# Layer 0's product of batches 1 to 3 on four column groups, with the row sums taken from added-up weights and the maximum in a PSUM bank of its own

## The chip, the core and the metric

The kernel runs on one core of a Trainium2 chip. A core has five engines that run side by side, each through its own list of instructions in order: PE (TensorE, matrix products into PSUM), DVE (VectorE), ACT (ScalarE), POOL (GpSimd) and SP (SyncE, here only for issuing DMAs). They wait for each other through semaphores. PSUM, the memory that PE writes, has 8 banks of 2 KB in each of 128 partitions. The metric is the device time of one execution in microseconds, the median of a few runs; a profiled execution also gives a trace of every instruction.

## What is computed

All data is fp32. `x` has 4 batches of 256 tokens with 512 features, and each batch has a context of 1601 rows of 512. Two layers follow each other, each a cross attention and a feed-forward step, all added onto `x`:

```python
x = x + _L0_xattn_ref(_layernorm(x), ctx_4096, ...)   # latent attention, 16 heads of 32
x = x + _L0_ffn_ref(_layernorm(x), ...)               # int4 weights, dequantized
x = x + _L1_xattn_ref(_layernorm(x), ctx_4096, ...)   # 16 heads of 96, 4 key/value heads
x = x + _L1_ffn_ref(_layernorm(x), ...)               # low-rank experts, gated
```

The change lies in layer 0's attention:

```python
C_kv = K @ Wkv_d                                      # context rows -> 32 latents
scores = einsum('bnhl,bkl->bhnk', CqWqk, C_kv) / sqrt(32)
attn = softmax(scores)
out = einsum('bhnk,bkhd->bnhd', attn, (C_kv @ Wv_u) per head)
```

The kernel uses that the keys' latents are shared by all heads: per head it forms `latents^T @ weights` (32 by 256) and only then multiplies by `Wv_u`. The softmax's sums come from the same product, with columns of ones beside the latents.

## The kernel before, in words

**Heads.** There are 4 batches times 16 heads in each of two layers, 128 heads in all, and each runs the same steps in `Head.schedule`. The 1601 context rows of layer 0 are 13 tiles of 128 (the last one overlaps, and its repeated rows are masked to zero); layer 1 has 15, with the 256 tokens themselves. The tiles of a head lie in four groups (4, 4, 3, 2 for layer 0, order `ORDER0`; 4, 4, 4, 3 for layer 1), each a tile `S` of up to 128 by 4 by 256 of which 8 exist, enough for two heads.

**Steps of a head.** PE writes scores to PSUM (layer 0: `Head0.score_units`, L1406; layer 1: L1483), four matmuls of 32 rows at a time on four row groups of the array. ACT copies each group to `S` (L1272). DVE takes running maxima over the tiles (L1290, L1293, L1298) into `mx`. PE transposes `mx` (L1321, the "turn") into a PSUM tile `om`, DVE reduces it to one maximum per query (L1325), PE transposes that back, broadcast over all partitions (L1334, the "spread"), into the other half of the same tile, and DVE copies it to SBUF as `mB` (L1342). DVE subtracts `mB` from each of the four groups (L1351), ACT exponentiates them (L1360), and PE multiplies them with the values (layer 0: L1433, layer 1: L1508), accumulating in the first half of `om`. ACT copies the result out (layer 0: `oT`, L1450; layer 1: L1547 to L1553).

**Layer 0's product.** The stationary operand of a tile is 64 wide: 32 latents and 32 ones (`ckv`). Even tiles go to columns 0 to 63 of the array, odd tiles to 64 to 127, so two matmuls stand side by side: 13 matmuls in 7 steps. `l0_output` (L778) adds the two halves up by multiplying `oT` with `wv_h`, which holds `Wv_u` at rows 0 and 64 and a one at rows 32 and 96 to pick the sums; DVE divides (L789, L790) and POOL adds to `x` (L808).

**PSUM.** Scores have two tiles of two banks (`s_psum`), `om` has two tiles of one bank (`o_psum`, tag "o"), and all other products two of one bank (`aux_psum`).

**Order of the work.** Nothing runs in the order in which the program names it. Every step is a `task` with an engine, an assumed duration, dependences, a priority and the buffers that it takes; `Plan.forward` places tasks one at a time where they can start earliest, the priority deciding between equals, and `Plan.order` repeats that with priorities computed backwards and keeps the best of nine rounds. The `AT_` constants shift the first round's priorities of each kind of step; `HOLD` is added to a PE task whose tiling of the array ("form": full, 32 rows, 64 columns, ...) is not the one in use. The result is a fixed list for each engine. `LINE` sets the order of heads: 16 of layer 0 of batch 0; then three stages that mix the 16 layer-1 heads of a batch with the 16 layer-0 heads of the next; then the 16 layer-1 heads of batch 3. Beside the heads PE makes keys (L895), values (L837), queries (L986), output products (L1096) and the feed-forward products (L610).

**Start.** ACT's queue issues loads of `x`, small weights and `wv_h` (L262 to L308) ahead of its first computation (L513); POOL sets constants (L255 to L345) ahead of its first power (L486), which the first layer norm waits for.

## Time and profile before

| what | us |
|---|---|
| median of 3 runs | 1981.87 (1981.84 to 1982.26) |
| the profiled execution | 1979.79 |
| its span, first to last instruction | 1978.0 |
| PE busy in it | 1905.7 (96%), 14745 matmul records |
| DVE busy | 1379.7 (70%), 2086 instructions |
| ACT busy | 1158.3 (59%) |
| POOL busy | 119.4 (6%) |
| mean granted TensorE clock | 0.982 |

One fp32 matmul of the program leaves two records in the trace, so 26 records of a layer-0 product are its 13 matmuls. A group row gives line, engine, operation, output and inputs, shapes and count, then busy time and mean duration in ns, then the idle time of the engine just before such instructions and what ended it. A timeline row gives start and length in us and merges neighbours of one line. A window row gives the length of a stretch, and for each engine its busy time and number of instructions in it.

### The profile page before, as it was taken

To read this page: it belongs to the slowest core of one execution; us is meant where nothing else is said; L and a number is where in the kernel's file an instruction comes from. 1 tells how busy PE (TensorE), PEld (TensorE's weight loads), DVE (VectorE), ACT (ScalarE), POOL (GpSimd) and SP (SyncE) were. 2 spreads that over 40 slices of the span, in tenths; PEclk is the share of its full clock that TensorE was granted. 3 is DMA by queue.
4 is the path that set the end of the run, shared out by engine and by line. 5 is a ranking of instruction groups with operands and counts; after the bars stand their busy time and mean duration, and the time that the engine had idled before them with its cause. 6 is when DMAs were issued, how large, how long until landed. Compare 5 with 4: busy or idle time off the path is not lost. (4 is left out here: it accounts for less than half of the span.)

```text
span 1978.0 us, 35851 instructions
## 1 busy us (share of the span) xinstructions
PE 1905.7 (96%) x14745; PEld 1336.7 (68%) x14745; DVE 1379.7 (70%) x2086; ACT 1158.3 (59%) x1752; POOL 119.4 (6%) x171
## 2 busy tenths in 40 slices
PE   6999899999999998999999999999999999999976
PEld 4566677666767776666666786666676678777743
DVE  3987458888887355888887636588879655577743
ACT  3887356776776434667776533567677654455530
POOL 1001200000001000000000100000000010000000
PEclk9999999999999999999999999999999999999986
DMA  7000432211000315220101024212100012221121
GB/s 196 16 12 28 149 86 57 62 38 36 23 9 23 86 54 151 54 62 28 38 15 30 22 65 142 79 50 57 41 25 17 23 46 57 68 70 45 45 60 42
DMA packets 132871, 109.11 MB, mean 55 GB/s; under 512 B 69059, under 2 KB 110179, under 8 KB 132324
## 3 DMA queue, kind: packets, MB, share of 16 engines
q1 hardware_dynamic: 125332, 96.01, 17.6%
q10 hardware_dynamic: 7376, 10.82, 1.7%
q8 instruction: 116, 1.90, 0.4%
q14 instruction: 47, 0.39, 0.1%
HBM read 93.50 MB, written 13.27 MB: 54 GB/s over the span
## 5 line engine op out<-in xcount | busy, mean ns | idle before, releaser
L1272 ACT COPY S<-s 128x1024 f32<-128x1024 f32 (+2 forms) x512 | 447.5, 905 | 300.4 <-PE s L1483 150.0
L1360 ACT ACTIVATE S<-S 128x1024 f32<-128x1024 f32 (+2 forms) x512 | 472.7, 950 | 156.2 <-DVE S L1351 128.8
L1351 DVE TENSOR_TENSOR S<-S,mB 128x1024 f32<-128x1024 f32 (+2 forms) x512 | 544.9, 1109 | 4.4
L1293 DVE TENSOR_TENSOR mx<-mx,S 128x512 f32<-128x512 f32 (+1 forms) x704 | 464.2, 659 | 113.4 <-ACT S L1272 87.2
L1508 PE MATMUL o<-S,v 128*97 128x256 f32 x1920 | 458.6, 382 | 0.6 <-ACT S L1360 0.6
L1508 PEld LDWEIGHTS o<-S,v 128*97 128x97 f32 x1920 | 302.2, 164 | 107.4 <-issue 22.9
L1483 PE MATMUL s<-q,kT_k_ps_c 32*128 32x256 f32 x4320 | 276.3, 383 | 0.0
L1483 PEld LDWEIGHTS s<-q,kT_k_ps_c 32*128 32x128 f32 x4320 | 224.6, 185 | 44.8 <-issue 19.5
L1433 PE MATMUL o<-S,ckv 128*64 128x256 f32 x1664 | 225.2, 389 | 1.5 <-ACT S L1360 1.3
L1433 PEld LDWEIGHTS o<-S,ckv 128*64 128x64 f32 x1664 | 117.0, 137 | 92.5 <-issue 31.2
L1290 DVE TENSOR_TENSOR mx<-S 128x512 f32<-128x512 f32 x128 | 88.7, 693 | 123.7 <-ACT S L1272 123.4
L837 PE MATMUL v_ps<-wvT_sb,ctxT 128*128 128x192 f32 x832 | 160.4, 336 | 0.0
L895 PE MATMUL k_ps_c<-ctxT,wk_sb 128*128 128x384 f32 (+1 forms) x480 | 159.2, 453 | 0.3 <-ACT kTlast_k_ps_c L905 0.3
L837 PEld LDWEIGHTS v_ps<-wvT_sb,ctxT 128*128 128x128 f32 x832 | 136.8, 192 | 22.5 <-issue 15.5
L1406 PE MATMUL s<-q,ckvT 32*128 32x256 f32 x1664 | 148.6, 409 | 0.0
L1406 PEld LDWEIGHTS s<-q,ckvT 32*128 32x128 f32 x1664 | 90.6, 185 | 54.7 <-issue 34.7
L1325 DVE TENSOR_REDUCE m<-o 128x2 f32<-128x256 f32 x128 | 53.5, 418 | 85.5 <-PE o L1321 84.8
L895 PEld LDWEIGHTS k_ps_c<-ctxT,wk_sb 128*128 128x128 f32 x480 | 79.1, 190 | 40.8 <-issue 13.7
L1096 PE MATMUL wo_ps<-wo,oT 128*128 128x512 f32 x192 | 93.6, 609 | 13.1 <-POOL oT L1083 13.1
L905 ACT COPY kT_k_ps_c<-k_ps_c 32x384 f32<-32x384 f32 (+1 forms) x180 | 76.7, 426 | 47.3 <-PE k_ps_c L895 44.8
L986 PE MATMUL q_ps<-xnT_xn_tp_a,wq 128*128 128x256 f32 x384 | 97.6, 386 | 1.9 <-ACT p_q_ps L995 1.9
L1483 PE MATMUL s<-q,kTlast_k_ps_c 32*128 32x256 f32 x1440 | 96.3, 391 | 0.0
(139 smaller groups left out, 1339.1 us busy)
## 6 DMA issues: line engine op xcount, KB each, us to landing
q<-q_rows SPq DMA_DIRECT2D x192, 96.0 KB
wq<-in_wqT SPq DMA_DIRECT2D x48, 192.0 KB
wo<-in_woT SPq DMA_DIRECT2D x16, 576.0 KB
q<-q_rows SPq DMA_DIRECT2D x128, 64.0 KB
ctxT<-in_ctxT ACTq DMA_DIRECT2D x6, 1024.0 KB
q_rows<-p_q_ps SPq DMA_DIRECT2D x48, 128.0 KB
q<-q_rows SPq DMA_DIRECT2D x192, 32.0 KB
rb<-rsums SPq DMA_DIRECT2D x16, 288.0 KB
```

The costliest lines, as they stand in the source:

```text
L837: nc.tensor.matmul(ps[:, : 2 * HD], lhsT=src.tile[:, c, a : a + P], rhs=wvT_sb[:, c, half * 2 * HD : (half + 1) * 2 * HD], start=(c == 0), ...
L895: nc.tensor.matmul(out, lhsT=wk_sb[:, c, i, :], rhs=rhs, start=(c == 0), stop=(c == NC - 1),)
L986: nc.tensor.matmul(ps[:, :T], lhsT=wq.tile[:, c, :], rhs=xnT.tile[:, c, :], start=(c == 0), stop=(c == NC - 1),)
L1096: nc.tensor.matmul(ps, lhsT=oT.tile[:, i, q * P : (q + 1) * P], rhs=wo.tile[:, i, :], start=(i == 0), stop=(i == G - 2),)
L1272: nc.scalar.copy(S4[g].tile[:, :n, :], self.scored(ps[g].tile, g))
L1293: nc.vector.tensor_tensor(mx.tile[:, :w, :], mx.tile[:, :w, :], t[:, a : a + w, :], ALU.max)
L1351: nc.vector.tensor_tensor(s[:, :n, :], s[:, :n, :], mb.tile[:, None, :].to_broadcast([P, n, T]), ALU.subtract,)
L1360: nc.scalar.activation(s[:, :n, :], s[:, :n, :], AF.Exp, scale=self.scale)
L1406: nc.tensor.matmul(pss[2 * step + r // 2][:, 2 * (r % 2) + s % 2, :], lhsT=st8[self.b]["ckvT"].tile[part, s, :], rhs=qr[part, self.h % 2, ...
L1433: nc.tensor.matmul(po[64 * par : 64 * par + 64, :], lhsT=s["ckv"].tile[:, t, :, :].rearrange("p o l -> p (o l)"), rhs=self.S[g].tile[:, i, :],
L1483: nc.tensor.matmul(pss[2 * step + r // 2][:, 2 * (r % 2) + slot % 2, :], lhsT=s["kT", self.kv].tile[part, c, slot, :], rhs=s["q1", self.kv ...
L1508: nc.tensor.matmul(po[:VW, :], lhsT=s["v", j // 2].tile[:, t, j % 2, :], rhs=self.S[g].tile[:, i, :], start=(k == 0), stop=(k == NK1 - 1),)
```

## The change

For batches 1 to 3 (`Head0.packed`) layer 0's product uses four column groups of 32. Three of them take the latents of three tiles at a time; 13 tiles make five steps (`units_of_three`). The fourth takes ones as the stationary operand, and as the moving operand a tile of weights in which several tiles have been added up: `add_up` puts the sum of groups 0 and 1 into the two free slots of group 3 (`S[3]`, slots 2 and 3), and tiles 8, 9 and 10 into the free slot of group 2; `TERMS` names the five operands (tiles 11 and 12 go in as they are) and which addition each must wait for. That makes 18 matmuls in 5 steps for 13 in 7, and five new DVE additions for each head. `l0_output` then needs a second set of `Wv_u`, `wv_3`, with rows 0, 32 and 64, beside `wv_2`. Batch 0 keeps the old product.

For all 128 heads the turn and the spread go to a PSUM tile of their own (tag "m", one), the product to another (tag "o", now one), and the four subtractions read the spread maximum from PSUM; the copy to `mB` is gone. Priorities are rounded, `HOLD` is 2.0, all `AT_` constants are new, and there is one more, `AT_SUM`, for the additions. Two blocks of definitions only move to another place; they are left out here.

```diff
@@ -66,7 +66,7 @@
     SWITCH = 0.2
-    HOLD = 1.0
+    HOLD = 2.0
     def __init__(self):
         self.tasks = []
...
@@ -74,7 +74,7 @@
     def task(self, eng, us, what, deps=(), prio=0.0, new=(), uses=(), lag=0.0, form="full"):
-        t = Task(eng, us, what, [d for d in deps if d is not None], prio, new, len(self.tasks))
+        t = Task(eng, us, what, [d for d in deps if d is not None], round(prio, 4), new, len(self.tasks))
         t.lag, t.form = lag, form
         for b in (*new, *uses):
             b.users.append(t)
...
@@ -243,11 +243,19 @@
     def s_psum(name):
         return psum.tile([P, 4, T], F32, tag="s", bufs=2, name=name)
+    def m_psum(name):
+        return psum.tile([P, 2, T], F32, tag="m", bufs=1, name=name)
     def o_psum(name):
-        return psum.tile([P, 2, T], F32, tag="o", bufs=2, name=name)
+        return psum.tile([P, 2, T], F32, tag="o", bufs=1, name=name)
     def aux_psum(name):
         return psum.tile([P, 512], F32, tag="aux", bufs=2, name=name)
+    FULL = S // P
+    DUP = (FULL + 1) * P - S
...
@@ -302,13 +310,18 @@
     first_ctx = load_ctx(0, nc.sync, load_wv)
-    wv_h = const.tile([P, H0, 33], F32, name="wv_h")
-    nc.gpsimd.memset(wv_h, 0.0)
-    for r in (0, 64):
-        nc.scalar.dma_start(
-            out=wv_h[r : r + L0, :, 0:32], in_=wv_u.rearrange("l (h d) -> l h d", d=32)
-        )
-        nc.gpsimd.memset(wv_h[r + 32 : r + 33, :, 32:33], 1.0)
+    wv_h = []
+    for name, rows, picks in (("wv_2", (0, 64), (32, 96)), ("wv_3", (0, 32, 64), (96,))):
+        w = const.tile([P, H0, 33], F32, name=name)
+        nc.gpsimd.memset(w, 0.0)
+        for r in rows:
+            nc.scalar.dma_start(
+                out=w[r : r + L0, :, 0:32], in_=wv_u.rearrange("l (h d) -> l h d", d=32)
+            )
+        for r in picks:
+            nc.gpsimd.memset(w[r : r + 1, :, 32:33], 1.0)
+        wv_h.append(w)
...
@@ -778,7 +787,7 @@
                 nc.tensor.matmul(
                     ps[:, (2 * q + j) * 33 : (2 * q + j + 1) * 33],
                     lhsT=oTs[j].tile[:, q * P : (q + 1) * P],
-                    rhs=wv_h[:, 2 * pair + j, :],
+                    rhs=wv_h[Head0.packed(b)][:, 2 * pair + j, :],
                     start=True,
                     stop=True,
                 )
...
@@ -1208,26 +1217,27 @@
-    AT_KEYS = -4.0
-    AT_VALUES = -3.0
-    AT_HALF = 1.5
-    AT_QUERY = -3.2
-    AT_LATENT = -2.8
-    AT_START0 = -5.4
-    AT_W0 = 0.6
-    AT_OUT = -2.0
-    AT_EVICT = -0.2
-    AT_SCORES = -3.0
-    AT_COPY = -0.9
-    AT_MAX = -1.8
-    AT_TURN = -0.9
-    AT_SPREAD = -0.5
-    AT_SUB0 = -0.8
-    AT_SUB1 = -1.0
-    AT_EXP0 = -0.2
-    AT_EXP1 = -0.4
-    AT_PROD = 0.2
-    AT_FIN = -2.8
+    AT_KEYS = -2.9
+    AT_VALUES = -0.2
+    AT_HALF = 1.7
+    AT_QUERY = -7.6
+    AT_LATENT = -9.3
+    AT_START0 = -16.1
+    AT_W0 = -4.1
+    AT_OUT = 0.9
+    AT_EVICT = 1.6
+    AT_SCORES = -2.5
+    AT_COPY = 4.3
+    AT_MAX = -4.3
+    AT_TURN = -2.8
+    AT_SPREAD = 0.7
+    AT_SUB0 = 4.6
+    AT_SUB1 = -6.6
+    AT_EXP0 = -10.3
+    AT_EXP1 = -19.9
+    AT_SUM = 11.8
+    AT_PROD = 0.3
+    AT_FIN = -8.1
     class Head:
         chains = {"scores": None, "copy": None, "product": None}
...
@@ -1240,7 +1250,7 @@
             at, chains = self.at, self.chains
             S4 = self.S = [Buf("S", 8) for _ in range(4)]
             ps = [Buf("s", 2) for _ in range(4)]
-            mx, om, mb = Buf("mx", 2), Buf("o", 2), Buf("mB", 1)
+            mx, om, po = Buf("mx", 2), Buf("m", 1), Buf("o", 1)
             copied = []
             for groups, units in self.score_units():
...
@@ -1315,7 +1325,7 @@
             t = task("DVE", tt(T), last_maximum, [t], at + AT_SPREAD, uses=[mx])
             def turn():
-                om.tile = o_psum(f"o{self.name}")
+                om.tile = m_psum(f"pm{self.name}")
                 for q in range(NQ):
                     half = slice(q * P, (q + 1) * P)
                     nc.tensor.transpose(om.tile[:, 0, half], mx.tile[:, 0, half], ident)
...
@@ -1337,21 +1347,16 @@
                         ident,
                     )
-            def keep():
-                mb.tile = work.tile([P, T], F32, tag="mB", bufs=1, name=f"mB{self.name}")
-                nc.vector.tensor_copy(mb.tile, om.tile[:, 1, :])
             t = task("PE", 0.24, turn, [t], at + AT_TURN, [om], [mx])
             t = task("DVE", 0.43, over_keys, [t], at + AT_SPREAD, uses=[om])
             t = task("PE", 0.24, spread, [t], at + AT_TURN, uses=[om])
-            t = task("DVE", 0.43, keep, [t], at + AT_SPREAD, [mb], [om])
             def subtract(g):
                 n, s = self.groups[g], S4[g].tile
                 nc.vector.tensor_tensor(
                     s[:, :n, :],
                     s[:, :n, :],
-                    mb.tile[:, None, :].to_broadcast([P, n, T]),
+                    om.tile[:, 1:2, :].to_broadcast([P, n, T]),
                     ALU.subtract,
                 )
...
@@ -1363,27 +1368,46 @@
             for g in range(4):
                 n = self.groups[g] * T
                 t = task(
-                    "DVE", tt(n), lambda g=g: subtract(g), [t], at + (AT_SUB0 if g < 2 else AT_SUB1), uses=[S4[g], mb]
+                    "DVE", tt(n), lambda g=g: subtract(g), [t], at + (AT_SUB0 if g < 2 else AT_SUB1), uses=[S4[g], om]
                 )
                 weighed.append(
                     task("ACT", cp(n) + 0.05, lambda g=g: weights(g), [t], at + (AT_EXP0 if g < 2 else AT_EXP1), uses=[S4[g]])
                 )
+            self.weighed = weighed
+            self.add_up(S4)
+            first = True
             for us, groups, deps, uses, what in self.product_units():
+                def run(what=what, first=first):
+                    if first:
+                        po.tile = o_psum(f"o{self.name}")
+                    what(po.tile[:, 0, :])
                 chains["product"] = t = task(
                     "PE",
                     us,
-                    lambda what=what: what(om.tile[:, 0, :]),
+                    run,
                     [chains["product"], *(weighed[g] for g in groups), *deps],
                     at + AT_PROD,
-                    uses=[om, *(S4[g] for g in groups), *uses],
+                    [po] if first else (),
+                    [*([] if first else [po]), *(S4[g] for g in groups), *uses],
                     form=self.product_form,
                 )
-            self.finish(om, t)
+                first = False
+            self.finish(po, t)
     class Head0(Head):
         layer, groups, scale = 0, [4, 4, 3, 2], 1.0 / math.sqrt(L0)
-        product_form = "64 columns"
+        def __init__(self, b, h, at):
+            super().__init__(b, h, at)
+            self.product_form = "32 columns" if self.packed(b) else "64 columns"
+        @staticmethod
+        def packed(b):
+            return b > 0
         def score_deps(self):
             s = st8[self.b]
...
@@ -1419,7 +1443,52 @@
                 for step, slots in enumerate(((0, 1), (2, 3)))
             ]
+        PARTS = [
+            (3, slice(2, 4), [(0, slice(0, 2)), (0, slice(2, 4))]),
+            (3, slice(2, 4), [(1, slice(0, 2)), (1, slice(2, 4))]),
+            (2, slice(3, 4), [(2, slice(0, 1)), (2, slice(2, 3)), (3, slice(0, 1))]),
+        ]
+        TERMS = [(3, 2, 0, 1), (3, 3, 0, 1), (2, 1, FULL, None), (3, 1, 0, None), (2, 3, 0, 2)]
+        def add_up(self, S4):
+            self.added = []
+            if not self.packed(self.b):
+                return
+            begun = set()
+            for to, where, parts in self.PARTS:
+                first = to not in begun
+                begun.add(to)
+                def run(to=to, where=where, parts=parts, first=first):
+                    own = S4[to].tile[:, where, :]
+                    terms = [S4[g].tile[:, at, :] for g, at in parts]
+                    if first:
+                        nc.vector.tensor_tensor(own, terms[0], terms[1], ALU.add)
+                        terms = terms[2:]
+                    for term in terms:
+                        nc.vector.tensor_tensor(own, own, term, ALU.add)
+                n = (where.stop - where.start) * T
+                groups = sorted({to, *(g for g, _ in parts)})
+                self.added.append(
+                    task(
+                        "DVE",
+                        (len(parts) - first) * tt(n),
+                        run,
+                        [*self.added[-1:], *(self.weighed[g] for g in {g for g, _ in parts})],
+                        self.at + AT_SUM,
+                        uses=[S4[g] for g in groups],
+                    )
+                )
         def product_units(self):
+            return self.units_of_three() if self.packed(self.b) else self.units_of_two()
+        def units_of_two(self):
             run = [(t, g, i) for g, o in enumerate(ORDER0) for i, t in enumerate(o)]
...
@@ -1442,6 +1511,32 @@
                 groups = sorted({half[k][1] for half in halves if k < len(half)})
                 yield mm(T), groups, s["ckv_done"], [s["ckv"]], lambda po, k=k: unit(k, po)
+        def units_of_three(self):
+            run = [(t, g, i) for g, o in enumerate(ORDER0) for i, t in enumerate(o)]
+            s = st8[self.b]
+            def unit(k, po):
+                steps = [
+                    (s["ckv"].tile[:, t, 0, :], self.S[g].tile[:, i, :], k == 0, 3 * k + r + 3 >= NK0)
+                    for r, (t, g, i) in enumerate(run[3 * k : 3 * k + 3])
+                ]
+                g, i, t, _ = self.TERMS[k]
+                total = (s["ckv"].tile[:, t, 1, :], self.S[g].tile[:, i, :], k == 0, k == 4)
+                for r, (lhsT, rhs, start, stop) in [*enumerate(steps), (3, total)]:
+                    nc.tensor.matmul(
+                        po[32 * r : 32 * r + 32, :], lhsT=lhsT, rhs=rhs, start=start, stop=stop
+                    )
+            for k in range(5):
+                g, _, _, after = self.TERMS[k]
+                groups = {g, *(x for _, x, _ in run[3 * k : 3 * k + 3])} if after is None else {x for _, x, _ in run[3 * k : 3 * k + 3]}
+                deps, uses = s["ckv_done"], [s["ckv"], self.S[g]]
+                if after is not None:
+                    deps = [*deps, self.added[after]]
+                yield mm(T), sorted(groups), deps, uses, lambda po, k=k: unit(k, po)
         def finish(self, om, t):
             oT = st8[self.b]["oT0", self.h] = Buf("oT0", 2)
...
@@ -1456,6 +1551,9 @@
     class Head1(Head):
         layer, groups, scale = 1, [4, 4, 4, 3], 1.0 / math.sqrt(HD)
         product_form = "full"
+        def add_up(self, S4):
+            pass
         def __init__(self, b, h, at):
             super().__init__(b, h, at)
```

## The prediction

> **What bounds the kernel now.** I read the page's busy times first, then the table of stretches, then the timeline of PE and of DVE for what one step costs.
>
> ```profile
> PE 1905.7 (96%) x14745; PEld 1336.7 (68%) x14745; DVE 1379.7 (70%) x2086; ACT 1158.3 (59%) x1752; POOL 119.4 (6%) x171
> ```
>
> PE is never long without work, but 70% for DVE is a mean over unlike stretches. In the table (PE, PEld, DVE, ACT, POOL busy in each stretch) the rows from 280, 800 and 1280 us hold most layer-0 heads of batches 1 to 3, those from 610 and 1090 almost none:
>
> ```profile
> 70.00:190.00 120.00, 119.87 (x872) 75.41 (x872) 100.29 (x159) 98.68 (x161) 7.12 (x14) 1.00 0.05 15
> 280.00:610.00 330.00, 328.11 (x2672) 225.31 (x2664) 273.91 (x399) 232.34 (x327) 15.59 (x22) 1.00 0.15 38
> 610.00:760.00 150.00, 145.99 (x1037) 109.67 (x1036) 81.12 (x131) 64.69 (x115) 12.21 (x14) 0.99 0.27 78
> 800.00:1090.00 290.00, 287.83 (x2326) 195.64 (x2322) 241.15 (x352) 202.67 (x290) 15.18 (x22) 0.99 0.15 39
> 1090.00:1240.00 150.00, 143.92 (x1004) 107.69 (x996) 80.98 (x131) 64.85 (x116) 12.23 (x14) 0.99 0.27 79
> 1280.00:1565.00 285.00, 283.11 (x2270) 192.00 (x2269) 239.36 (x350) 201.32 (x288) 15.23 (x21) 0.99 0.15 39
> ```
>
> Where the change takes work from PE, DVE is at 83 to 84% already; where it touches nothing, at 54%. What a step costs stands in the timeline, as the distance to the next row's start:
>
> ```profile
> 768.85 3.68 PE L637 MATMUL ckv_ps<-ctxT,wkv_d_sb 128*32 128x128 f32 x104
> 772.47 0.71 PE L1483 MATMUL s<-q,kTlast_k_ps_c 32*128 32x256 f32 x6
> ...
> 908.35 1.95 PE L1433 MATMUL o<-S,ckv 128*64 128x256 f32 x16
> 910.22 0.43 PE L1334 MATMUL o<-ident,m 128*128 128x128 f32 x2
> ...
> 940.60 3.24 PE L1433 MATMUL o<-S,ckv 128*64 128x256 f32 x26
> 943.76 1.15 PE L1406 MATMUL s<-q,ckvT 32*128 32x256 f32 x16
> ```
>
> Layer 0's product: 16 records (4 steps of two matmuls) take 1.87 us, 26 (7 steps) 3.16, so a step is 0.43 (0.4317 in the trace's starts) and a run costs 0.15 besides. Of that, 0.093 is the change of form: successive starts at 256 columns are 0.309 us apart across one and 0.216 within a form. The row at 768.85 is the only work on four column groups: 52 matmuls of 128 columns, 12 steps of four and 4 singles, 16 steps of 0.216, which is 3.45; it took 3.62. So four stand side by side at full pace.
>
> ```profile
> 87.99 0.42 DVE L1342 COPY mB<-o 128x256 f32<-128x256 f32 x1 [0.86 <-PE o L1334]
> 88.44 3.23 DVE L1351 TENSOR_TENSOR S<-S,mB 128x1024 f32<-128x1024 f32 x3
> 91.59 1.94 DVE L1293 TENSOR_TENSOR mx<-mx,S 128x512 f32<-128x512 f32 x3
> 93.57 0.43 DVE L1298 TENSOR_TENSOR mx<-mx 128x256 f32<-128x256 f32 x1
> 93.91 0.69 DVE L1351 TENSOR_TENSOR S<-S,mB 128x512 f32<-128x512 f32 x1
> 94.51 0.68 DVE L1290 TENSOR_TENSOR mx<-S 128x512 f32<-128x512 f32 x1
> ```
>
> On DVE a 512 operation takes 0.61 of the engine (0.73 if the next one reads its result), a 256 one 0.34 (0.46), three subtractions 3.15 (1.136, 1.136, 0.869), the copy 0.45.
>
> **The change part by part.** *PE's product.* 48 heads go from 7 steps to 5: 48 x 2 x 0.4317 = 41.4 us less, all on PE. *Forms.* In the instruction lists the form on PE changes 752 times before and 730 after: 22 x 0.093 = 2.0 less. Adding each matmul's columns and each change of form along the lists gives 1845.0 us for before and 1801.6 after, 43.4 less. Measured was a span of 1978.0, so 133 us were waits and small gaps.
>
> *DVE.* The copy goes: 128 x 0.45 = 58 less. The additions come: per head three of 512 and two of 256, between 2.5 (0.61, 0.34) and 3.1 us (0.73, 0.46); along the list, where some follow each other, 2.8; 48 x 2.8 = 134 more. Layer-0 heads of batches 1 to 3 rise from 9.0 to 11.3 us of DVE, others fall by 0.45. *Subtractions from PSUM.* The addition that reads PSUM (L602, 128x512) took 680 ns, the like maximum from SBUF (L1290) 693; nothing is added. [...]
>
> *Where the sums fall.* I cut the lists at the turns and added up both engines between them. "Dense" are positions 20 to 44, 52 to 76 and 84 to 108 of the heads' order. Dense: PE 810 before and 810 after, as other PE work was moved in; DVE 710 and 800; measured before 835, 3.1% over PE. First 12 heads: PE 113 and 112, DVE 110 and 105, measured 119, 5.3% over. Next 8: PE 142 and 138, measured 153. Sparse stretches at 44 and 76: PE 377 and 348, DVE 205 and 208, measured 398. From 108 on: PE 343 and 336, measured 344. Ends: 59 and 57, measured 128.
>
> Dense after thus has DVE at 99% of PE, and the row it is nearest to is the first 12 heads, at 98%: 5.3%, so 810 x 1.053 = 853, 18 more than before. First 12, now at 93%: 4% over, 117, 2 less. The next 8 and the sparse stretches, with their waits as measured (11 and 21), 4 and 29 less. From 108 on 8 less, ends 2 less. Sum: +18 - 2 - 4 - 29 - 8 - 2 = -27.
>
> *The wait on the additions.* The product's first step needs the sum of groups 0 and 1, so two subtractions, two exponentials and three additions: queued behind it on PE are the next heads' scores, and ACT's copies and DVE's maxima wait for those. Between spread and first product the list holds 8.4 us of other PE work (median; 4.9 before), against 1.14 + 1.14 for the subtractions, 1.06 for the last exponential and about 2 for the additions, 5.4. It fits while DVE is on time; that is inside the 5.3%, and DVE itself now stands behind ACT's exponentials.
>
> *One bank each.* The turn must wait for the last subtraction of the head before: 3.75 us of DVE, and the list never puts less than 5.3 of PE work there. A product must wait for ACT's copy (0.37, for layer 1 twice, and up to 1.06 of an exponential in front): at least 1.27 us lie between, under 2.0 in 9 of 127 places. Bounds: 0 to 9 x 0.6 = 5; I take 0, the median being 5.1.
>
> *Start.* POOL sets a second constant ahead of the first layer norm: 0.54 of memset and 0.12, +0.6 us. ACT's queue gets three more loads, 0.65 each, which wait for that memset (about 13 us in); its first copy came at 16.96 after 7.5 idle, so they lie beside. Bounds 0 to 2; 0.6, inside the rounding above. SP issues the same DMAs.
>
> The forecast is 1981.9 - 27 = 1955 (the profiled span was 1978.0 and its execution 1979.8, 2 under the median).
>
> **The rivals.** *The whole PE gain comes through.* DVE keeps up, dense stays at 3.1%: 18 less than the forecast, 1937. For it: before, four-head cuts with DVE at 83 to 92% of PE lost 1 to 3%. Against: at 93% one lost 6%, another 10%.
>
> *DVE takes over and the kernel gets slower.* If dense loses 10%, as the worst four heads before did (41.7 of PE in 45.9), it takes 891, 38 more than forecast: 1993. It decides from 8.6% (853 + 27 = 880). For it: new waits of DVE on ACT and of PE on DVE in the same stretch, with S buffers for two heads only. Against: the first 12 heads ran at equal load, ACT above 80% too, at 5.3%.
>
> *Four groups don't run side by side at 256 columns.* If only pairs did, 18 matmuls are 9 steps, not 7: 41 more instead of 41 less, 82 over the forecast, 2037. Against it stands the row at 768.85. [...]
>
> **How the numbers follow.** Forecast 0.5; full PE gain 0.22; DVE takes over 0.17; no fourfold product 0.03; the rest, 0.08, is a wash or a stall that I haven't named. A change under 0.2% (4 us) can't be told from none. Faster holds the first two and a little of the rest: 0.74; same 0.05; slower 0.21. Low end: full gain and 5 us off the waits, 1932; high end: most of the way to the slower rival, 1988. The forecast's own range is 1943 to 1970.
>
> **What would show it.** Right: the new product's group (1728 records) at about 48 x 2.31 = 111 us busy, additions near 140, subtractions still near 1239 ns, DVE near 1470, and the former rows 280 to 610 and the like with DVE above 90%, hardly shorter than before, while those from 610 and 1090 shrink by some 15 us each. Wrong: PE waits on the additions or on ACT's exponentials, more than 20 us over the run (slower rival); steps of four longer than 0.45; subtractions above 1300 ns; or PE at 98% in the dense stretches (full gain).

## The result and the profile after

The changed kernel takes 1967.1 us (median; 1966.8 to 1970.7) against 1981.9 before, a ratio of 0.993 with a 95% interval of 0.9913 to 0.9947. It is 14.8 us faster; 27 had been forecast (1955). The number lies inside the forecast's own range (1943 to 1970) and the sign is right, but nearly half of the expected gain is missing, and the experiments below ask where it went.

The profiled execution after has a span of 1965.0 us (1978.0 before) at the same mean granted clock, 0.982. Its first line of busy times:

```profile
PE 1871.3 (95%) x15225; PEld 1305.0 (66%) x15225; DVE 1447.0 (74%) x2198; ACT 1152.0 (59%) x1752; POOL 110.3 (6%) x173
```

PE is busy 34 us less and DVE 67 more. The table of stretches of the changed kernel (length, then PE, PEld, DVE, ACT, POOL busy, granted clock, DMA share, GB/s), cut to the nearest us where the dense stretches begin and end, with the two sparse ones last:

```profile
313.00:594.00 281.00, 277.89 (x2463) 188.27 (x2462) 260.29 (x391) 200.53 (x290) 11.44 (x21) 1.00 0.14 36
783.00:1066.00 283.00, 278.47 (x2457) 187.49 (x2456) 262.91 (x393) 195.76 (x282) 11.96 (x21) 1.00 0.15 40
1253.00:1537.00 284.00, 279.30 (x2459) 187.99 (x2458) 264.45 (x394) 196.48 (x283) 12.04 (x21) 1.00 0.15 40
594.00:783.00 189.00, 178.57 (x1374) 131.27 (x1373) 106.45 (x168) 86.88 (x147) 11.36 (x16) 0.98 0.28 79
1066.00:1253.00 187.00, 178.55 (x1389) 132.33 (x1388) 104.07 (x166) 91.21 (x156) 11.36 (x16) 0.99 0.27 77
```

and the same stretches of the kernel before:

```profile
317.50:595.00 277.50, 275.61 (x2249) 186.84 (x2249) 234.50 (x344) 196.59 (x277) 14.98 (x21) 1.00 0.15 39
794.00:1073.00 279.00, 276.83 (x2254) 188.35 (x2253) 235.73 (x344) 196.19 (x276) 14.64 (x21) 0.99 0.14 37
1272.00:1550.50 278.50, 276.61 (x2253) 188.27 (x2252) 235.56 (x344) 195.73 (x276) 14.60 (x21) 0.99 0.14 37
595.00:794.00 199.00, 193.02 (x1430) 143.36 (x1429) 105.57 (x167) 93.13 (x162) 12.96 (x17) 0.98 0.27 78
1073.00:1272.00 199.00, 192.66 (x1429) 143.25 (x1428) 105.36 (x167) 93.00 (x162) 12.91 (x17) 0.98 0.27 78
```

DVE is busy 93% of the dense stretches, as forecast, and PE has 3 to 5 us without a matmul in each (2 before). In the sparse ones PE has 8 to 10 (6 before).

The prediction's sum can be set beside the measurement stretch by stretch, since both cut at the turns of the same heads. "List" is PE's own work added up along its instruction list:

| stretch (heads in order) | list before, after | measured before, after | change | forecast |
|---|---|---|---|---|
| first 12 | 113, 112 | 119.0, 119.1 | +0.1 | -2 |
| 12 to 20 | 142, 138 | 153.3, 146.1 | -7.2 | -4 |
| dense | 810, 810 | 835.2, 848.3 | +13.1 | +18 |
| sparse | 377, 348 | 398.1, 375.5 | -22.6 | -29 |
| from 108 on | 343, 336 | 344.2, 346.9 | +2.7 | -8 |
| ends | 59, 57 | 128.2, 129.0 | +0.9 | -2 |

The clock column matters for the dense row. The trace's clock records hold 6.8 us at half clock in the dense stretches before (the two that show 0.99) and none after. Half of that time is lost, 3.4 us, so at full clock the dense stretches went from 831.8 to 848.3, by 16.5. That this is the right way to take the clock out is seen in two runs below that leave the dense stretches' work as it is (the weights loaded once, the merged loads). They take 850.5 and 853.3 there with 3.4 and 10.2 us at half clock, which leaves 848.8 and 848.2 for the 848.3 of the changed kernel.

The shortfall is mostly in two rows: 11 us from turn 108 on, 6 in the sparse stretches. What PE waits for there stands in its list of waits (what waits, for what, us in total, times, longest). After:

```profile
PE wo_ps L1105 <- POOL oT L1092: 18.7, 5, 12.3
PE q_ps L995 <- DMA wq<-in_wqT: 12.8, 10, 3.2
...
PE pm L1331 <- DVE mx L1308: 5.8, 8, 1.3
...
PE o L1528 <- DVE S L1473: 1.0, 3, 0.6
```

and the same view of the kernel before:

```profile
PE wo_ps L1096 <- POOL oT L1083: 13.1, 1, 13.1
PE o L1321 <- DVE mx L1298: 10.0, 9, 2.0
...
PE cq_ps L698 <- ACT p_q_ps L995: 5.6, 2, 2.9
```

The product hardly waits for its additions (1.0 us). New is a wait that the prediction did not have: layer 1's query product waits ten times for its weights `wq` to land, 12.8 us, and the output product waits five times instead of once for the round trip behind `oT`. From turn 108 to the last turn all of PE's listed waits are 7.5 us, 4.2 of them on `wq`, where the kernel before has 0.7.

The subtractions and the additions in the groups of the changed kernel, shapes kept apart (busy, mean ns, idle before):

```profile
L1356 DVE TENSOR_TENSOR S<-S,pm 128x1024 f32<-128x1024 f32 x320 | 377.1, 1215 | 34.1 <-PE pm L1344 33.0
...
L1473 DVE TENSOR_TENSOR S<-S,S 128x512 f32<-128x512 f32 x96 | 68.0, 708 | 5.7 <-ACT S L1365 0.2
...
L1470 DVE TENSOR_TENSOR S<-S 128x512 f32<-128x512 f32 x48 | 32.8, 683 | 0.0
...
L1473 DVE TENSOR_TENSOR S<-S,S 128x256 f32<-128x256 f32 x48 | 20.4, 426 | 4.9
L1470 DVE TENSOR_TENSOR S<-S 128x256 f32<-128x256 f32 x48 | 20.0, 417 | 0.0
```

The subtractions of the kernel before, which read the maximum from SBUF:

```profile
L1351 DVE TENSOR_TENSOR S<-S,mB 128x1024 f32<-128x1024 f32 x320 | 383.0, 1239 | 4.4
```

The new product, again in the changed kernel:

```profile
L1528 PE MATMUL o<-S,ckv 128*32 128x256 f32 x1728 | 125.8, 384 | 1.0 <-DVE S L1473 1.0
```

The additions are 141 us (140 forecast). The product is 125.8 instead of 111, because other work cuts many products in two (the 48 products run in 93 pieces), as PE's timeline of the changed kernel shows (start, length):

```profile
875.20 1.93 PE L1528 MATMUL o<-S,ckv 128*32 128x256 f32 x32
878.35 0.62 PE L1528 MATMUL o<-S,ckv 128*32 128x256 f32 x4
```

Those are the 36 records of one product in two pieces. The nine uncut products take 2.296 us each between its first start and the next work's, which is 5 x 0.4317 + 0.138: the steps of four run at the forecast pace.

### The profile page after: what moved, and what is told of

Same layout as the page of the kernel before. It is cut to its first block, busy times and chain, and to the rows that moved or that the text cites. A ratio compares the mean times of both kernels' runs of the same rounds, so it can differ in the third digit from the quotient of the medians.

```text
span 1965.0 us, 37125 instructions
## 1 busy us (share of the span) xinstructions
PE 1871.3 (95%) x15225; PEld 1305.0 (66%) x15225; DVE 1447.0 (74%) x2198; ACT 1152.0 (59%) x1752; POOL 110.3 (6%) x173
## 5 line engine op out<-in xcount | busy, mean ns | idle before, releaser
L1282 ACT COPY S<-s 128x1024 f32<-128x1024 f32 (+2 forms) x512 | 445.1, 907 | 315.9 <-PE s L1581 153.3
L1303 DVE TENSOR_TENSOR mx<-mx,S 128x512 f32<-128x512 f32 (+1 forms) x704 | 473.0, 672 | 112.4 <-ACT S L1282 84.1
L1356 DVE TENSOR_TENSOR S<-S,pm 128x1024 f32<-128x1024 f32 (+2 forms) x512 | 528.4, 1081 | 34.1 <-PE pm L1344 33.0
L1528 PE MATMUL o<-S,ckv 128*32 128x256 f32 x1728 | 125.8, 384 | 1.0 <-DVE S L1473 1.0
L1105 PE MATMUL wo_ps<-wo,oT 128*128 128x512 f32 x192 | 100.1, 643 | 18.7 <-POOL oT L1092 18.7
L995 PE MATMUL q_ps<-xnT_xn_tp_a,wq 128*128 128x256 f32 x384 | 101.8, 397 | 13.4 <-DMA wq<-in_wqT 12.8
L1335 DVE TENSOR_REDUCE m<-pm 128x2 f32<-128x256 f32 x128 | 53.8, 421 | 62.7 <-PE pm L1331 62.6
L1473 DVE TENSOR_TENSOR S<-S,S 128x512 f32<-128x512 f32 x144 | 88.4, 614 | 10.6 <-ACT S L1365 0.2
L995 PEld LDWEIGHTS q_ps<-xnT_xn_tp_a,wq 128*128 128x128 f32 x384 | 71.0, 195 | 35.1 <-issue 17.5
```

The source lines that it names most:

```text
L995: nc.tensor.matmul(ps[:, :T], lhsT=wq.tile[:, c, :], rhs=xnT.tile[:, c, :], start=(c == 0), stop=(c == NC - 1),)
L1105: nc.tensor.matmul(ps, lhsT=oT.tile[:, i, q * P : (q + 1) * P], rhs=wo.tile[:, i, :], start=(i == 0), stop=(i == G - 2),)
L1282: nc.scalar.copy(S4[g].tile[:, :n, :], self.scored(ps[g].tile, g))
L1303: nc.vector.tensor_tensor(mx.tile[:, :w, :], mx.tile[:, :w, :], t[:, a : a + w, :], ALU.max)
L1356: nc.vector.tensor_tensor(s[:, :n, :], s[:, :n, :], om.tile[:, 1:2, :].to_broadcast([P, n, T]), ALU.subtract,)
L1528: nc.tensor.matmul(po[32 * r : 32 * r + 32, :], lhsT=lhsT, rhs=rhs, start=start, stop=stop)
```

## The experiments

Ratios are to the kernel before, on the same chip and in the same minutes, with 95% intervals; the changed kernel's own is 0.993.

### Which part brings the gain: the product or the constants

The packed product taken back, with the banks and the constants kept:

```diff
-            return b > 0
+            return b > B
```

> The changed kernel with all batches on the old product (13 matmuls in 7 steps, no additions); the banks, the subtractions from PSUM and the new constants stay, and the plan is made anew. Along its lists PE adds up to 1841 us instead of 1802, DVE to 1317 instead of 1455; in the dense stretches PE 831 and DVE 676. Theory (the additions load DVE so that part of PE's gain is lost in the dense stretches): dense falls to about 3% over its PE, 856, that is 8 more than the changed kernel's 848, and the rest follows PE; the time is 25 to 32 us above the changed kernel's 1967, near 1995. Rival A (DVE costs nothing, PE's sum alone counts): 39 us more, 2006. Rival B (the gain came from the constants and the banks, the product gave nothing): within 5 us of 1967.

Measured: 1986.4 us, ratio 1.0028 [1.0018, 1.0039], 19 us above the changed kernel: short of the theory's 25 to 32 and of rival A's 39, but far from rival B, by which the product gains nothing. The dense stretches took 855.1 us, as the theory said. And the product and the banks kept, with `HOLD` and all `AT_` constants as before:

```diff
-    HOLD = 2.0
+    HOLD = 1.0
-    AT_KEYS = -2.9
+    AT_KEYS = -4.0
...
-    AT_SUB0 = 4.6
-    AT_SUB1 = -6.6
+    AT_SUB0 = -0.8
+    AT_SUB1 = -1.0
...
```

> The changed kernel with the former AT constants and HOLD 1.0 (AT_SUM at -0.2); the plan is made anew. Along its lists PE adds up to 1805 us, DVE to 1453, dense 814 and 795: nearly the changed kernel's sums. Theory (the sums decide, and waits as in the kernel before stay where they were): dense 4.7% over PE, 852, the rest near before's waits; 1960 to 1972. Rival (the gain is mostly the constants'): 1978 or more.

Measured: 1987.2 us, ratio 1.0032 [1.0014, 1.005]; the theory missed by 15 us and the rival held. Neither half gains anything: each alone is 0.3% slower than before. The third part, the banks with the subtractions from PSUM, stands in both runs, and no run takes it back. Given the new constants, the packed product is worth 0.98%, 19 us, while PE's list is 39 us shorter by it (1841.1 and 1801.6). With the old constants the stretch from head 12 to 20 takes 172 us instead of 146, though PE's list there is only some 8 longer; its trace holds 20.5 us at half clock there, 10 us of the 26.

### Is the loss in the dense stretches DVE's load

The additions left out, at the same order of every engine:

```diff
-        TERMS = [(3, 2, 0, 1), (3, 3, 0, 1), (2, 1, FULL, None), (3, 1, 0, None), (2, 3, 0, 2)]
+        TERMS = [(3, 0, 0, 1), (3, 1, 0, 1), (2, 1, FULL, None), (3, 1, 0, None), (2, 2, 0, 2)]
...
-                    if first:
-                        nc.vector.tensor_tensor(own, terms[0], terms[1], ALU.add)
-                        terms = terms[2:]
-                    for term in terms:
-                        nc.vector.tensor_tensor(own, own, term, ALU.add)
+                    return
```

> Leaves out the five additions per head; the product takes slots that are there anyway, so the sums of the softmax are not those of the reference. All other instructions stand in the same order on every engine. DVE loses about 134 us, 90 of them in the dense stretches, PE stays at 1802. Theory (the dense stretches lie 4.7% over PE because DVE is at 99%): dense falls from 848 to about 835 (3.1% over PE, as before the change), 13 us less, and the time is near 1953. Rival (the 4.7% comes from the order itself, each chain waiting for PE and ACT): dense stays at 845 or more, time within 4 us of 1967.

Measured: 1963.8 us, ratio 0.991 [0.9895, 0.9925]. DVE's list in the dense stretches fell from 800 to 672 us and they went from 848.3 to 845.9. As measured the theory missed and the rival held, by a narrow margin. But the clock hides part of the effect:

```profile
314.00:597.00 283.00, 279.57 (x2462) 189.32 (x2462) 221.63 (x316) 200.22 (x289) 11.23 (x21) 0.99 0.14 36
785.00:1067.00 282.00, 278.47 (x2458) 188.00 (x2457) 226.62 (x318) 195.62 (x282) 12.02 (x21) 0.99 0.15 41
1257.00:1538.00 281.00, 277.64 (x2462) 188.03 (x2461) 226.69 (x318) 195.93 (x282) 11.72 (x21) 1.00 0.16 41
```

Two of these stretches hold 3.4 us at half clock each, where the changed kernel has none. Without that loss the three take 842.5, so 5.8 us go with the additions, less than half of what the theory expected. The edit also makes the product's first step read group 3, and PE waits 0.7 us for it in the first stretch, so 5.8 is rather a little too low. Then the other way, with the copy of the maximum put back on DVE:

```diff
+                kept = S4[2 + self.layer].tile[:, 3:4, :]
+                if g == 0:
+                    nc.vector.tensor_copy(kept, om.tile[:, 1:2, :])
...
-                    om.tile[:, 1:2, :].to_broadcast([P, n, T]),
+                    kept.to_broadcast([P, n, T]),
```

> The changed kernel with the spread maximum copied to SBUF again, into a free slot of S, and subtracted from there; the order stays. Each head has 0.45 us more on DVE: along the list 838 in the dense stretches, 28 more than PE. Theory (DVE was not what set the dense stretches at 800, but has no more than some 5% to give): it takes over, 838 at about 95% is 875 to 885, and the time is 20 to 40 us above the changed kernel, 1987 to 2007. Rival (DVE still hides, only the chain of each head gets 0.45 longer): below 1975.

Measured: 2002.8 us, 1.011 [1.0094, 1.0126]. And with the additions made twice:

```diff
-                    for term in terms:
+                    for term in [*terms, *(S4[g].tile[:, at, :] for g, at in parts)]:
```

> Adds the terms a second time into the same slots, so the sums are wrong; the order stays. DVE gains seven operations per head of batches 1 to 3, and along the list has 993 us in the dense stretches against PE's 810. Theory (past PE's sum DVE sets the time): dense 1030 to 1050, about 190 more, time near 2155. Rival (a second half is still hidden beside PE): below 2000.

Measured: 2165.4 us, 1.0929 [1.0905, 1.0954]. The theory held in both. All these runs and the changed kernel have one order of PE's list, 810 us in the dense stretches, and so give their time against DVE's list alone:

| DVE's list, us | 672 | 800 | 838 | 993 |
|---|---|---|---|---|
| dense, us | 845.9 | 848.3 | 874.0 | 1035.8 |
| of it at half clock, us | 6.8 | 0 | 6.8 | 95.6 |
| dense / DVE's list | | | 1.043 | 1.043 |

In this order 128 us of DVE's list below the change are worth 2.4 us as measured and 5.8 at full clock, and the 38 us above it cost 26. The two heavier runs take 1.043 times DVE's list; that line meets 848 at a list of some 812, an estimate, as no run lies between 800 and 838. By it the change stands 12 us below the point where DVE sets the time. So "DVE at 99% of PE" explains about a third of the 16.5 us by which the dense stretches grew, and not the whole. The next candidate was ACT, whose exponentials were halved:

```diff
-                nc.scalar.activation(s[:, :n, :], s[:, :n, :], AF.Exp, scale=self.scale)
+                nc.scalar.activation(s[:, :n, : T // 2], s[:, :n, : T // 2], AF.Exp, scale=self.scale)
```

> Exponentiates only the first half of each group's columns, so the weights of the other half are wrong; the order stays. ACT loses about 1.5 us per head, some 190 us, and the way from subtraction to product gets 0.4 shorter. Theory (what keeps the dense stretches 4.7% over PE's sum is ACT, or the time that a chain spends there): dense falls from 848 to 825 or 835, time 1945 to 1955. Rival (they are small stalls that PE has by itself at changes of form and at weight loads with a wait): dense 843 or more, time within 5 us of 1967.

Measured: 1958.7 us, 0.9886 [0.9867, 0.9906]; dense 846.7 with nothing at half clock, so for these stretches the rival held (1.6 us less). Most of the 8 us came from elsewhere, 3 from the sparse ones and 2 from turn 108 on. Last, both edits at once, and as a control the half exponentials in the kernel before:

> The changed kernel without the five additions of a packed head (its fourth column group then multiplies parts of the weights as they are) and with layer 0's and layer 1's exponentials over half of the queries alone, the order of every engine kept. The sums and the other half of the weights are left out. VectorE's list in the dense stretches is 672 us instead of 800, and ScalarE's busy time about a fifth less. Each of the two edits alone left the dense stretches at 846 and 847 us against 848. Theory (what the dense stretches lose beyond TensorE's list of 810 lies in the order of TensorE's own queue, short stalls from its own chain, and no other engine's load feeds it): dense 841 to 847 together, time 1950 to 1960. Rival (VectorE and ScalarE cover for one another: each alone is late only where the other is too): dense at most 833, time at most 1945.

> The kernel before the change with the exponentials of both layers over half of the queries alone, the order of every engine kept; the other half of the weights is left out. It is the control to the changed kernel without additions and with half the exponentials, whose dense stretches fell from 848 to 839 us, though each of the two edits alone left them at 846 and 847. Theory (the change's additions and the exponentials behind them cover for one another in stalls that the kernel before does not have): the dense stretches before go from 835 to 832 or more, and the time falls by less than 6 us (1975 or more). Rival (the exponentials cost the dense stretches as much in the kernel before too, and what the changed kernel lost there comes from the order of TensorE's own list): dense at most 828, time at most 1971.

Measured: both at once 1956.5 us, 0.9877 [0.986, 0.9894], a time inside the theory's range, and dense 838.6, between the two bounds, with nothing at half clock. The control: 1980.4 us, 0.9996 [0.9987, 1.0006], dense 834.8 against 835.2, each with 6.8 us at half clock; there the theory held. The middle dense stretch of both edits, and that of the control:

```profile
778.00:1057.00 279.00, 276.15 (x2460) 187.45 (x2459) 227.12 (x318) 164.02 (x283) 11.73 (x21) 1.00 0.15 41
```
```profile
797.00:1076.00 279.00, 276.84 (x2256) 188.72 (x2255) 234.89 (x344) 164.66 (x276) 14.54 (x21) 0.99 0.14 37
```

At full clock the dense stretches lost 16.5 us. Of these 5.8 go without the additions, 1.6 with half the exponentials, and 9.7 with both, 2.3 more than the two together: the additions are the larger part, and each of the two covers a little for the other. In the kernel before, shorter exponentials change nothing there. That the loss sits in the chain from subtraction over exponential and addition to product fits this, and no run shows it step by step. The other 6.8 us stay open; the new order of PE's list is a candidate that no run isolates. The median times show less of the joint effect (1956.5 against 1958.7 for the exponentials alone, with overlapping intervals), as the trace with both edits is that of the fastest of four executions, which reach 1960.0.

### The waits for the query weights

`wq` loaded once and not 48 times:

```diff
-                wq.tile = work.tile([P, NC, P], F32, tag="wq", bufs=2, name=f"wq_{b}_{kv}_{i}")
+                if "wq tile" in book:
+                    wq.tile = book["wq tile"]
+                    return
+                book["wq tile"] = wq.tile = const.tile([P, NC, P], F32, name="wq_once")
```

> Leaves out all but the first load of layer 1's query weights (94 DMAs fewer on SP's queue, 45 us of its issue time; all heads then use the first weights). The order of all other instructions stays. Theory (the new PE waits after the dense stretches, 12.8 us on these loads and some 5 us on the scaled oT, come from SP's queue, where loads stand behind each other at 0.4 to 0.5 us each): PE no longer waits for the weights, the stretches from head 44, 76 and 108 lose 12 to 18 us together, and the time is 1950 to 1955. Rival (PE would wait there anyway, for ACT or DVE, the weights are only what came last): 1963 or more.

Measured: 1952.3 us (four runs from 1946.9 to 1959.4), 0.9853 [0.9828, 0.9879]; the theory held, but for the wait behind `oT`, which stayed (19.1 us). The sparse stretches went from 375.5 to 365.9 and the part from turn 108 on from 346.9 to 343.0. Most of the missing gain hangs on these loads; from 108 on they give back 4 of the missing 11 us. To see whether SyncE's time to issue them is to blame, 192 of its other DMAs were merged, three of 128 partitions in place of four of 32 for a query, and one in place of four for its last part:

```diff
-                for r in range(4):
+                rows4 = far[:HD].rearrange("(c l) t -> l c t", l=32)
+                for c in range(3):
                     nc.sync.dma_start(
-                        out=t[32 * r : 32 * r + 32],
-                        in_=far[:HD].rearrange("(c l) t -> l c t", l=32),
+                        out=t[:, c, :],
+                        in_=rows4[None, :, c, :].to_broadcast([4, 32, T]),
                     )
...
-                for r in range(4):
-                    nc.sync.dma_start(
-                        out=q1[G - 1].tile[32 * r : 32 * r + 32, i, :], in_=far[HD:P]
-                    )
+                nc.sync.dma_start(
+                    out=q1[G - 1].tile[:, i, :],
+                    in_=far[HD:P][None, :, :].to_broadcast([4, 32, T]),
+                )
```

> The changed kernel, but layer 1's queries are brought to the four row groups by three loads, or one, that write all 128 partitions, in place of four (192 DMAs fewer on SP's queue, about 88 us of its issue time at 0.46 each). All other instructions stand in the same order, and the output is the reference's. Theory (SP's queue brings the query weights, and through them PE, late): PE's waits for the weights (12.8 us) and for the scaled oT after the dense stretches shrink, and the time is 1950 to 1957. Rival (a load of 128 rows takes SP or the DMA engines four times as long, so nothing comes earlier): 1963 or more.

Measured: 1990.8 us, 1.0054 [1.0036, 1.0072]: not 10 us faster but 24 slower than the changed kernel. Its first wait of PE and a piece of its timeline:

```profile
PE q_ps L995 <- DMA wq<-in_wqT: 23.8, 7, 3.9
```
```profile
668.85 1.63 SPq L1013 DMA_DIRECT2D q<-q_rows  x3
...
670.26 1.89 PE L995 MATMUL q_ps<-xnT_xn_tp_a,wq 128*128 128x256 f32 x8
...
670.58 0.42 SPq L988 DMA_DIRECT2D wq<-in_wqT  x1
...
671.05 0.51 SPq L992 DMA_DIRECT2D wq<-in_wqT  x1
...
676.32 3.53 PE L995 MATMUL q_ps<-xnT_xn_tp_a,wq 128*128 128x256 f32 x8 [3.31 <-DMA wq<-in_wqT]
```

The same place in the changed kernel:

```profile
664.77 1.75 SPq L1012 DMA_DIRECT2D q<-q_rows  x4
...
666.61 0.39 SPq L988 DMA_DIRECT2D wq<-in_wqT  x1
...
667.05 0.51 SPq L992 DMA_DIRECT2D wq<-in_wqT  x1
...
669.78 1.97 PE L995 MATMUL q_ps<-xnT_xn_tp_a,wq 128*128 128x256 f32 x8 [0.92 <-DMA wq<-in_wqT]
```

From the second issue to the product's start it is 2.7 us behind four narrow loads and 5.3 behind three wide ones; in the ten waits of the changed kernel it is 2.5 to 2.8, in the seven of this run 5.3 to 6.4. SyncE's issue time for the queries' loads fell from 161 to 101 us, so the time in the queue, not the issuing, makes the weights late. What in the queue is slower behind wide loads, no run shows. And a second price is seen in the lengths: eight records of that product take 1.89 us, but 3.53 after the wait of 3.31. The clock in the table of stretches says why; first this run, then the changed kernel, where the ten records of the output product took 7.61 us after a wait of 3.55:

```profile
676.00:680.00 4.00, 3.68 (x10) 2.98 (x11) 0.00 (x0) 0.07 (x1) 0.00 (x0) 0.57 0.48 134
680.00:684.00 4.00, 4.00 (x32) 3.51 (x34) 1.75 (x1) 1.63 (x5) 0.15 (x1) 1.00 0.19 63
```
```profile
690.00:698.00 8.00, 7.52 (x11) 3.14 (x12) 4.09 (x7) 0.00 (x0) 0.43 (x1) 0.58 0.04 12
698.00:706.00 8.00, 8.00 (x97) 6.55 (x98) 4.11 (x8) 3.04 (x4) 0.69 (x1) 1.00 0.29 85
```

Between the first and the last turn the trace's clock records hold 20.5 us at half clock before the change, 13.7 after, 47.8 in this run. The 34 more cost up to 17 us and the longer waits 11, which covers the 24. Of the 47.8, 10.2 us lie in the dense stretches behind waits of 1.2 us that the changed kernel has as well, without half clock, so that part is chance.

Could the planner have put the query product later? One number altered, the assumed landing time:

```diff
-            book["wq"] = t = task("SP", 0.2, load, [book["wq"]], prio - 1, [wq], lag=kb(256))
+            book["wq"] = t = task("SP", 0.2, load, [book["wq"]], prio - 1, [wq], lag=kb(256) + 2.0)
```

> The changed kernel with one number of the plan altered: the landing time that the planner assumes for a load of layer 1's query weights is 2.0 us longer (kb(256) + 2.0, so 4.85 us instead of 2.85). The work is the same, and the lists' sums are the same but for their split: TensorE 1801.7 us in all as before the edit, dense stretches 806 instead of 810, sparse stretches with the heads around them 356 instead of 348. Theory (TensorE waits 12.8 us for these weights in ten places because the plan puts the product too close behind the load, and this, with the changed order around it, is what ate the missing gain of the sparse stretches and of the end): the waits of q_ps on wq are below 4 us, and the time is 1950 to 1960. Rival (the waits are only where a delay shows that other queues cause, such as SyncE's own order; with the product put later, something else is late instead): waits on wq may go, but the time is 1964 to 1975.

Measured: 1966.5 us, 0.9929 [0.9912, 0.9945]. The waits on `wq` fell from 12.8 to 4.0 us, the sparse stretches by 4 and the end by 2, and the first 12 heads gained 5, but from head 12 to 20 it lost 6 and in the dense stretches 2 (3.4 us at half clock there account for most of it). And with SyncE's measured durations in the plan (`own` and `third` 1.85, the loads of `wq` 0.95 and of `wo` 0.85, the ways out 0.42 and 0.5, the way back 1.8):

```diff
-                done[0] = [task("SP", 0.3, own, [t, book.get("q1 new")], prio, [a], lag=3.0)]
+                done[0] = [task("SP", 1.85, own, [t, book.get("q1 new")], prio, [a], lag=3.0)]
...
-        t = task("SP", 0.3, back, [t], prio, [rb], lag=3.5)
+        t = task("SP", 1.8, back, [t], prio, [rb], lag=3.5)
```

> The changed kernel with the durations of SyncE's tasks in the plan set to what the trace of the changed kernel shows for their DMA issues (own and third part of a query 1.85 us instead of 0.3, a load of query weights 0.95 instead of 0.2, the outputs' way back 1.8 instead of 0.3, ways out 0.42 and 0.5 instead of 0.1, output weights 0.85 instead of 0.2). The work is the same; lists: TensorE 1802.4 us (dense 819, sparse 345, from turn 108 on 333), VectorE 1457. Theory (the plan lets TensorE meet layer 1's products before their loads and round trips have landed, because SyncE's time is missing in it): waits on wq and on the outputs' round trip shrink, time 1947 to 1960. Rival (a plan's order decides by other things, above all by how evenly the dense stretches are filled, and these get 9 us longer on the list): time 1963 or more.

Measured: 1969.7 us, 0.9943 [0.9929, 0.9958]. The wait for `oT` is back to a single one, and `wq` no longer stands among the longest:

```profile
PE xn_tp_a L514 <- DVE xn_a L504: 16.5, 1, 16.5
PE wo_ps L1105 <- POOL oT L1092: 12.0, 1, 12.0
PE o L1606 <- ACT S L1365: 9.0, 10, 2.1
```

The sparse stretches take 354.3 us (375.5 in the changed kernel) and the end 341.1 (346.9): with the lists' 345 and 333, the gain that the prediction had looked for is there. But the dense stretches now take 877.8, for a list of 819 and the same DVE load; half clock (13.7 us) is 7 of the 29 us that they got longer. In both runs the rivals held: the plan can move this loss, and in these two plans it came back elsewhere. No kernel that computes everything was measurably faster than the changed one.

## Why the prediction was right or wrong

**PE's product and forms (-43).** Right. Steps of four last 0.4317 at 256 columns, and the last rival (no fourfold concurrency) is out: the nine uncut products took 2.296 us, five whole steps of four and 0.138.

**DVE's sum (+134 - 58).** Right: additions 141 us busy, the copy gone, DVE at 1447 where 1470 was forecast.

**Subtractions from PSUM (0).** Right: 1215 ns against 1239 from SBUF. The zero was read from one addition that reads PSUM (680 ns against 693), and that row was a good guide.

**Dense stretches (+18).** The size was near, +13 (16.5 at full clock), but the reason holds for a third of it at most, so the near hit is partly luck. The step took the row "at 98%", the first 12 heads, and read its 5.3% as the price of DVE's load. That row did not follow DVE: in the changed kernel it has 105 us of DVE for 110, and took 119.1 as before, where 117 had been forecast. In the dense stretches 5.8 us go with the additions and 9.7 with half the exponentials besides; 6.8 stay at 672 us of DVE, which a sum per engine can't show. DVE's load becomes the limit just beyond where the change puts it, by the estimate at some 812 us.

**Sparse stretches (-29) and from 108 on (-8).** Here the step failed: "with their waits as measured", and a list shorter by 8 taken for 8 us. The waits that were there went (the heads from 48 and 80 on took 19.3 us more than their list before, 5.4 after); in their place PE met `wq` ten times before it had landed. Without those loads 15 us come back, more than the 12 by which the time missed 1955. The prediction counted that SP issues the same DMAs, and they are the same; what changed is how close behind them PE's list puts their readers. In the trace before, no query product starts less than 4.3 us after the second issue of its weights; in the changed kernel 11 of 48 start within 3.4. That could have been read in the two instruction lists. What is left from 108 on, some 7 us, is made up of several short waits and 1.7 us of half clock, and no run takes it apart.

**Start, banks, waits on additions (0 to +1).** Right within 1 to 3 us: PE waited 1.0 us for additions, and the turns' wait for DVE's maxima even fell (10.0 to 5.8).

**The rivals.** The slower one's mechanism is real and close by: 38 us more of DVE in the dense stretches (the copy kept) gave 874 there, near the 880 from which it was to decide, and a run slower than before. By the estimate the change ended 12 us of DVE short of it. Its price of 10%, from the worst four heads, was read too high: these heads (45.9 us) hold a piece of 3.4 us at half clock, and without it they lost 6%. The sign named for the full gain, PE at 98% in the dense stretches, came (98 to 99%) though they got longer; PE was at 99% there before, so it could not tell. The full gain needs two things that did not come together in any plan here: no waits in the sparse stretches and 3% over the list in the dense ones.

## What to carry to other kernels

When an ordered list is made anew, the engine sums tell what is possible; what came out here hung most on the distance between a load and its first reader (for `wq` 4.3 us or more before, within 3.4 for 11 of 48 after), so compare these distances in the two lists, load by load, for every queue. An engine's load cost little here while it lay below that of the bound engine (6 us for 128 of additions), and in full (1.04 us for each us of DVE) once it lay well above: find how far from that point a change ends before adding work there. Before two traces are compared stretch by stretch, take out what each lost at half clock; here that was more than half of an edit's effect. Test two suspected helpers of a stall together as well as singly, for each can cover for the other (here 5.8 and 1.6 us singly, 9.7 together).

## What the runs showed of the hardware

- Half clock came after waits of PE (of 1.62 to 3.55 us in the traces of the kernel before and of the changed one, between the first and the last turn), and the length of the wait alone did not decide. The same query product, after the same wait, ran at full clock in the changed kernel and partly at half clock in the run with the copy kept:

```profile
680.88 1.97 PE L995 MATMUL q_ps<-xnT_xn_tp_a,wq 128*128 128x256 f32 x8 [2.16 <-DMA wq<-in_wqT]
```
```profile
699.32 3.11 PE L995 MATMUL q_ps<-xnT_xn_tp_a,wq 128*128 128x256 f32 x8 [2.15 <-DMA wq<-in_wqT]
```

  Between the first and the last turn the pieces at half clock start, in every trace, on a grid of 3.41 us and last one or more whole steps of it. Counted there over all 14 traces, for grid steps at full clock: where PE stood still 2.0 us or more within one step, the next step was at half clock in 60 of 62 cases; at 1.5 to 2.0 us in 24 of 56; at 0.5 to 1.5 in 16 of 349; under 0.5 in none of 7018. So a wait that lies inside one step can cost more than a longer one that is split over two: 1.62 us inside one step (before, from 919.1) was followed by a step at half clock, 2.16 us in parts of 0.88 and 1.28 (after, from 678.5) by none. Half clock added 1.6 us to the eight records after waits of 3.31 and 3.87 us (3.53 instead of 1.89), and 3.1 to the ten of the output product after 3.55 (7.61 us; at full clock they took 4.56).
- Merging the queries' DMAs made them cheaper to issue (161 us in all for 384, 101 for 192) and slower for what stood behind them: from the next load's second issue to the product that waits for it, 5.3 to 6.4 us instead of 2.5 to 2.8.
- A subtraction that takes one operand from PSUM, spread over four tiles, cost no more than one that takes it from SBUF (1215 and 1239 ns at 1024 columns).
